# Sums over ordered rows by TensorE: two fp32r matmuls on a split operand in the place of one fp32 matmul

## The chip, the cores and the metric

The kernel runs on one core of a Trainium2 chip. The metric is the device time of one execution in microseconds (us). The time of the kernel before is the median of three runs, 2934.11 us. The engines are named as in the profile: PE is TensorE (matmuls and transposes), PEld its weight loads, DVE is VectorE, ACT is ScalarE, POOL is GpSimd, and SP issues most of the DMAs.

## The reference

Four graph-attention layers run over 32 independent graphs ("batches") of 512 nodes with 256 features, all in fp32. Each is `x = x + gat(relu(layernorm(x)))`. The last has two attentions inside, and the first of these has no mask. Cut to what matters here:

```python
def _gat(inp, adj_mask, W, a):
    h = jnp.matmul(inp, W)                       # (B, 512, 512) for this one
    f1 = jnp.matmul(h, a[:F_, 0])
    f2 = jnp.matmul(h, a[F_:, 0])
    e = jax.nn.leaky_relu(f1[:, :, None] + f2[:, None, :], ALPHA)
    if adj_mask is not None:
        e = jnp.where(adj_mask[None, :, :] > 0, e, NEG_INF)
    att = jax.nn.softmax(e, axis=2)
    return jax.nn.elu(jnp.einsum('bij,bjf->bif', att, h))
```

Without a mask, the weight of row j for node i depends only on whether `f1[i] + f2[j]` is positive: on one side it is one product of a factor of i and a factor of j, on the other side another. So if the rows of h are put in the order of f2, the whole attention of a node is one sum over the rows before a place in the order and one over the rows after it. The kernel uses this.

## The kernel before, in words

The 32 batches go through the layers in four streams (`NS = 4`), batch b in stream b mod 4. Each batch is a Python generator that hands over control at `yield`, and gives with it the time at which it wants to go on. `after_us` works this time out from a planner's count: `spent`, which `matmul` and `transpose` raise for every call, and a number of us written out by hand. A loop at the end always advances the stream whose time comes first. This fixes the order in which the program is written down. From there a scheduler sets the order of each engine's queue: instructions that were written earlier come first where their inputs are due by then, and others may be moved up in the meantime. A few DVE instructions are kept in the order written (`tc.keep_in_program_order`).

SBUF tiles come from pools by tag. Tiles of one tag share a fixed number of buffers, and a new one has to wait until the oldest is free. The tag `q` has three buffers of 2 x 256 fp32 values a partition. The ELUs of all streams use it: ACT writes an exponential into `q`, and DVE reads it. The tag `w` has four buffers. PSUM's eight banks are divided so that each active stream has two (`bank()`).

Batches 0 to 30 take the unmasked attention as `sort_attend`; batch 31 takes it as `attend`, with matmuls over the full weights. `sort_attend` does the following:

1. `project_half` makes the rows of h in two halves of 256 columns. Two more columns are put to each half, so that it has C = 258.
2. DVE and ACT count each row's place in the order. POOL scatters the rows to DRAM at those places (L607), and SP reads them back in order: partition p gets rows 4p to 4p+3 (`sums`, L614 and L615).
3. For each half, DVE adds up the four rows of a partition from the front (L627, L628) up to the total `tot` (L629). It then sums them from the back with factors (L630, L632) to `u`. PE carries these sums across partitions: `pv` is the sum of `tot` over all partitions before, by a triangle of 0 and 1 called `before` as the stationary operand. `pu` is the same with `u[:, 0, :]` over all partitions after, by `after`. ACT copies `pv` out (L640), DVE adds `pv` and `pu` to the rows (L641, L644, L646), and SP writes the result to a table in DRAM (L647, L648).
4. POOL gathers from the table the row that belongs to each node (L655), and DVE and ACT finish the attention (L670 to L675).

So the triangles are used twice for each half, four times a batch, and 31 batches make 62 matmuls with each. They are made once, in `setup`, which runs between the first steps of the streams. All matmuls in the profile appear on line 66, in the helper `matmul`, so they are told apart by their operands. The same holds for transposes (L70).

Of the other streams' work, what stands near the sums in the queues is the end of layer 2 (L405, L406), the normalization (L269 to L280), layer 1's factors and values (`both` L324, `v` L322 and L325), the attention weights `w` (L353), the first matmuls of layer 3 (`hT,WM`) and the weighted sums (`v,w`).

Of the kernel before, what the change touches and what calls it, by code (L numbers as in the profile page):

```python
# [18 lines left out]

FP = mybir.dt.float32  # L20
BF = mybir.dt.bfloat16
I32 = mybir.dt.int32
U32 = mybir.dt.uint32
AF = mybir.ActivationFunctionType
OP = mybir.AluOpType
# [3 lines left out]
P = 128  # L29
# [6 lines left out]
def fast(ctx, tc, flag, x, adj, w0, a0, w1, a1, w2, a2, mlp1_w, mlp1_b, mlp2_w, mlp2_b,  # L36
         w_fc, a_fc, w_hand, a_hand, out):
    nc = tc.nc
# [12 lines left out]
    const = ctx.enter_context(tc.tile_pool(name="const", bufs=1))  # L51
    work = ctx.enter_context(tc.tile_pool(name="work", bufs=2))
# [11 lines left out]
    def matmul(p, w, x, **flags):  # L64
        spent[0] += 4 * max(x.shape[-1], P)
        nc.tensor.matmul(p, w, x, **flags)  # L66

    def transpose(p, x, i, tied=False):
        spent[0] += 2 * P
        instruction = nc.tensor.transpose(p, x, i)  # L70
        if tied:
            tc.keep_in_program_order(instruction)
# [4 lines left out]
    def bank():  # L77

        own = [turn[0], *(i for i in range(NS) if i not in active and i != turn[0])]
        banks[0] += 1  # L80
        return psum.tile([P, N], FP, tag=f"b{own[banks[0] % len(own)]}", name="b", bufs=8 // NS)
# [46 lines left out]
    def fetch_w(w, a, name):  # L128

        kt, cols = w.shape[0] // P, w.shape[1]  # L130
        t = const.tile([P, kt, cols + 3], FP, name=name)
        wr = w.rearrange("(k p) f -> p k f", p=P)
        for c in range(0, cols, F):
            nc.sync.dma_start(t[:, :, c + (3 if c else 0):c + (3 if c else 0) + F], wr[:, :, c:c + F])
        return t, fetch_a(a, name + "a") if len(a.shape) == 2 else a

    def finish_w(fetched, alpha):
        t, a_cols = fetched

        def block(k, f):  # L140
            c = f * P + (3 if f * P >= F else 0)
            return t[:, k, c:c + P]

        scale_a(a_cols, alpha)
        for k in range(t.shape[1]):
            project(t[:, k, F:F + 3], block, k, a_cols)
            yield
# [4 lines left out]
    W0, _ = fetched0 = fetch_w(w0, a0_sb, "W0")  # L152
    adj_sb = work.tile([P, NT, N], I32, tag="w", name="adj", bufs=4)
    nc.sync.dma_start(adj_sb, adj.rearrange("(t p) j -> p t j", p=P))
# [24 lines left out]
    b2 = const.tile([P, KF], FP, name="bias2")  # L179
    diag = const.tile([P, NT], I32, name="diag")  # L180
    with nc.allow_non_contiguous_dma(reason="vectors onto partitions"):
# [4 lines left out]
    C = F + 2  # L186
# [8 lines left out]


    maskT = const.tile([P, NT, N], BF, name="maskT")
    before = const.tile([P, P], FP, name="before")
    after = const.tile([P, P], FP, name="after")
    band = const.tile([P, 2 * N - P], BF, name="band")  # L200
    differ = const.tile([P, 2], FP, name="differ")

# [4 lines left out]
    def setup():  # L207

        own = work.tile([P, NT, N], FP, tag="w", name="own", bufs=4)
        nc.vector.tensor_scalar(own, adj_sb, 0.0, None, op0=OP.is_gt)  # L210
        nc.gpsimd.affine_select(
            out=own, in_=own, pattern=[[P, NT], [-1, N]], base=0, channel_multiplier=1,
            compare_op=OP.not_equal, fill=1.0,
        )
        tc.keep_in_program_order(nc.vector.tensor_reduce(differ[:, 0:1], adj_sb, AX.XY, OP.min))
        nc.vector.tensor_scalar(differ[:, 0:1], differ[:, 0:1], 0.0, None, op0=OP.is_lt)
        for j in range(NT):
            turn[0] = NS - 1 - j % (NS - 1)
            p = bank()
            for t in range(NT):  # L220
                transpose(p[:, t * P:(t + 1) * P], own[:, t, j * P:(j + 1) * P], ident, j + t == 0)
            nc.scalar.copy(maskT[:, j, :], p)
        turn[0] = NS - 1
        yield
        yield from finish_w(fetched1, 0.01)


        least = small([1], "rden")
        nc.vector.tensor_reduce(least, diag, AX.X, OP.min)
        nc.vector.tensor_scalar(differ[:, 1:2], least, 0.0, None, op0=OP.is_le)  # L230
        nc.vector.tensor_copy(W2[:, :, :, :D], raw2.rearrange("p k (h d) -> p k h d", d=D))
        nc.vector.tensor_scalar_mul(A2v[:, :, 1:2], A2v[:, :, 0:1], -0.8)
        nc.vector.tensor_scalar_mul(A2v[:, :, 2:3], A2v[:, :, 2:3], 0.8)
        for k in range(KF):
            project(W2[:, k, :, D:], lambda k, f: raw2[:, k, f * P:(f + 1) * P], k, A2)
            yield
        yield from finish_w(fetched3, 0.2)

        for tri, sign in ((before, 1), (after, -1)):
            nc.vector.memset(tri, 1.0)  # L240
            nc.gpsimd.affine_select(
                out=tri, in_=tri, pattern=[[sign, P]], base=0, channel_multiplier=-sign,
                compare_op=OP.is_gt, fill=0.0,
            )
        ties = work.tile([P, 2 * N - P], FP, tag="w", name="ties", bufs=4)
        nc.vector.memset(ties, TINY)
        nc.gpsimd.affine_select(
            out=ties, in_=ties, pattern=[[-1, 2 * N - P]], base=N - P, channel_multiplier=1,
            compare_op=OP.is_gt, fill=0.0,
        )  # L250
        nc.vector.tensor_copy(band, ties)
        yield
        yield from finish_w(fetched4, 0.2)
# [277 lines left out]
    def attend(oT, b):  # L531
# [28 lines left out]
        mlp_in(oT, ys[-1], NT - 1)  # L560
        yield after_us(1)

    def sort_attend(oT, b):

        halves, ends = fc_values()
# [12 lines left out]
        p = bank()  # L578
# [5 lines left out]
        for t in range(NT):  # L584
            junk = work.tile([P, N], BF, tag="junk", name="junk", bufs=1)
            nc.vector.scalar_tensor_tensor(
# [10 lines left out]
        for t in range(NT):  # L597
            junk = work.tile([P, N], BF, tag="junk2", name="junk2", bufs=1)
            nc.scalar.activation(
# [4 lines left out]
        for c in range(2):  # L604
# [7 lines left out]
            u = flat[c].rearrange("p (t k) n -> p t k n", k=2)[:, :, 1, :]  # L612
# [6 lines left out]
        for c in range(2):  # L619
            yield sort  # L620
            sums = flat[c].rearrange("p (t k) n -> p t k n", k=2)
            u = sums[:, :, 1, :]

            T = small([NT], "T")
            tc.keep_in_program_order(nc.vector.tensor_copy(T, u[:, :, F + 1]))
            tot = work.tile([P, C], FP, tag="tot", name="tot", bufs=1)
            nc.vector.tensor_tensor(sums[:, 2, 0, :], u[:, 0, :], u[:, 1, :], op=OP.add)  # L627
            nc.vector.tensor_tensor(sums[:, 3, 0, :], sums[:, 2, 0, :], u[:, 2, :], op=OP.add)  # L628
            nc.vector.tensor_tensor(tot, sums[:, 3, 0, :], u[:, 3, :], op=OP.add)  # L629
            nc.vector.tensor_scalar_mul(u[:, 3, :], u[:, 3, :], T[:, 3:4])  # L630
            for t in (2, 1, 0):
                nc.vector.scalar_tensor_tensor(  # L632
                    u[:, t, :], u[:, t, :], T[:, t:t + 1], u[:, t + 1, :], op0=OP.mult, op1=OP.add
                )
            yield after_us(3)

            pv, pu = bank(), bank()
            matmul(pv[:, :C], before, tot, start=True, stop=True)
            matmul(pu[:, :C], after, u[:, 0, :], start=True, stop=True)
            nc.scalar.copy(sums[:, 0, 0, :], pv[:, :C])  # L640
            nc.vector.tensor_tensor(  # L641
                sums[:, 1:, 0, :], sums[:, 1:, 0, :], pv[:, None, :C].to_broadcast([P, NT - 1, C]), op=OP.add
            )
            nc.vector.tensor_tensor(u, u, pu[:, None, :C].to_broadcast([P, NT, C]), op=OP.add)  # L644
            q = 3 * P // 4
            nc.vector.tensor_tensor(tot[q:, :], tot[q:, :], pv[q:, :C], op=OP.add)  # L646
            nc.sync.dma_start(places[:, :, c, :], flat[c])  # L647
            nc.sync.dma_start(table[N:, c * C:(c + 1) * C], tot[P - 1:, :])  # L648
            sort = after_us(1)
# [14 lines left out]
        for t in range(NT):  # L664
            yield landed
            y, q = pair(), pair("q")
# [128 lines left out]
    p = bank()  # L795
# [7 lines left out]
def general(  # L803
# [52 lines left out]

    adj_sb = work.tile([P, NT, N], I32, tag="u", name="adj", bufs=4)
    nc.sync.dma_start(adj_sb, adj.rearrange("(t p) j -> p t j", p=P))
    m_pos = const.tile([P, NT, N], BF, name="m_pos")
    nc.vector.tensor_scalar(m_pos, adj_sb, 0.0, NEG, op0=OP.is_le, op1=OP.mult)  # L860
    m_nz = const.tile([P, NT, N], BF, name="m_nz")
    nc.vector.tensor_scalar(m_nz, adj_sb, 0.0, NEG, op0=OP.is_equal, op1=OP.mult)
# [335 lines left out]
def kernel(ctx: ExitStack, tc: tile.TileContext, *args):  # L1198
    nc = tc.nc
    keep = ctx.enter_context(tc.tile_pool(name="keep", bufs=1))  # L1200
    flag = keep.tile([1, 1], I32, name="flag")
    fast(tc, flag, *args)
# [30 lines left out]
```

## Time and profile before

| What | Value |
|---|---|
| Time, median of 3 runs | 2934.11 us (2930.95 to 2935.68) |
| Span of the profiled execution | 2929.6 us, 43083 instructions |
| The profiled execution's own time | not listed apart; the three runs' times are 1.4 to 6.1 us above the span |
| Granted TensorE clock over the span | 0.996 |
| POOL busy | 502.3 us, 515 instructions |
| Matmul records `b<-tot,before` and `b<-sums,after` | 124 each |
| Subtraction-like row: `tot` (L629), DVE, 128x258 fp32 | x62, median 421 ns |
| Copy of `pv` (L640), ACT, 128x258 fp32 from PSUM | x62, median 374 ns |
| Table writes (L647) | x62, 516 KB each |

The span goes from the first to the last instruction on the core. A row of the profile names the line, the engine, the operation, the tile written and the tiles read, the shapes and the count. After the bar come the busy time in us and the mean time of one in ns, and after a second bar the engine's idle time just before these instructions. PE's records overlap, since a matmul starts before the one ahead of it has ended; the time that PE gives to a matmul is read from the distance between starts. In a timeline the columns are start, duration, engine, line and operation, and in brackets the idle time before and what ended it. In the chain of waits the columns are start, length and the instruction.

### The profile page before, as it was taken

What the parts mean: (1) busy time and instruction counts of PE and PEld (TensorE: products, weight loads), DVE (VectorE), ACT (ScalarE), POOL (GpSimd) and SP (SyncE); (2) the same over time, 40 slices, a digit from 0 to 9 for tenths busy, and PEclk for the clock granted to TensorE, in tenths of its full rate; (3) what the DMA queues carried; (4) which work ended last, traced back from release to release, by engine and by line L of the source; (5) the groups of instructions that cost most, each with busy time, mean ns of one, the idle gap of its engine ahead of it and who ended that gap; (6) DMA issues with size and microseconds to landing.
All of it is one profiled execution on the core that took longest, in us unless ns stands there. A gap on an engine that the chain in (4) does not pass through costs nothing.

```text
span 2929.6 us, 43083 instructions
## 1 busy us (share of the span) xinstructions
PE 2858.9 (98%) x15177; PEld 2329.5 (80%) x15177; DVE 2219.9 (76%) x5676; ACT 1536.8 (52%) x3922; POOL 502.3 (17%) x515
## 2 busy tenths in 40 slices
PE   8999999999999999999999999999999999999998
PEld 6777887877888877888877888788887788877876
DVE  4677877778778778778778777787787787777764
ACT  4444455555555555555554556545555555555444
POOL 0011112112122111122021121111221111211220
PEclk9999999999999999999999999999999999999999
DMA  3033223233223333233332233222332322323230
GB/s 94 19 102 102 80 88 116 91 98 95 88 94 106 93 100 98 84 102 96 100 102 80 89 115 93 91 97 91 94 116 80 102 93 88 104 93 96 90 107 30
DMA packets 193182, 270.89 MB, mean 92 GB/s; under 512 B 17024, under 2 KB 156094, under 8 KB 192960
## 3 DMA queue, kind: packets, MB, share of 16 engines
q1 hardware_dynamic: 163200, 169.76, 18.5%
q0 software_dynamic: 29760, 98.30, 10.4%
q8 instruction: 123, 2.02, 0.3%
q14 instruction: 99, 0.81, 0.1%
HBM read 152.62 MB, written 115.39 MB: 91 GB/s over the span
## 4 chain that ended last, share of the span: by engine, by line
PE 82%; DVE 10%; ACT 4%; DMA 3%; issue 1%; SPq 0%; POOL 0%; DVEq 0%; POOLq 0%; ACTq 0%
PE b L66 75%; PE b L70 7%; DVE st L269 2%; DMA g<-table,at 2%; DVE sums L641 1%; DVE xn L280 1%; DVE x L406 1%; DVE y L405 1%; ACT v L325 1%; DVE sums L632 1%; ACT y L505 1%; ACT q L504 1%; DVE w L353 1%; ACT hT L290 1%; DVE tot L646 0%
## 5 line engine op out<-in xcount | busy, mean ns | idle before, releaser
L66 PE MATMUL b<-v,w 128*128 128x65 f32 (+1 forms) x7232 | 1218.0, 321 | 10.6 <-DVE w L353 10.5
L66 PEld LDWEIGHTS b<-v,w 128*128 128x128 f32 x7232 | 1050.0, 191 | 168.7 <-issue 56.1
L66 PE MATMUL b<-WFC,oT 128*128 128x256 f32 (+1 forms) x2048 | 495.2, 380 | 0.0
L66 PEld LDWEIGHTS b<-WFC,oT 128*128 128x128 f32 x2048 | 374.5, 189 | 49.3
L66 PE MATMUL b<-W,hT 128*128 128x259 f32 (+1 forms) x1536 | 388.8, 391 | 22.8 <-DVE v L463 14.1
L353 DVE SCALAR_TENSOR_TENSOR w<-b,v,maskT 128x512 f32<-128x512 f32 x512 | 369.4, 744 | 5.1 <-PE b L70 4.1
L607 POOL DMA_INDIRECT order<-v,at x248 | 277.0, 1117 | 490.7 <-DVE oT L730 152.3
L66 PEld LDWEIGHTS b<-W,hT 128*128 128x128 f32 x1536 | 285.3, 192 | 75.3 <-DVE v L463 17.1
L715 POOL TENSOR_TENSOR x<-x,y 128x512 f32<-128x512 f32 x62 | 87.8, 1416 | 1063.7 <-ACT y L713 950.0
L353 DVE SCALAR_TENSOR_TENSOR w<-spread,v,maskT 128x512 f32<-128x512 f32 x384 | 269.5, 742 | 0.0
L66 PE MATMUL b<-hT,WM 128*128 128x512 f32 x512 | 250.0, 599 | 0.7 <-ACT hT L290 0.7
L66 PE MATMUL b<-oT,WM 128*128 128x512 f32 x512 | 231.2, 594 | 0.0
L655 POOL DMA_INDIRECT g<-table,at x124 | 120.9, 975 | 642.8 <-ACT y L675 292.0
L387 DVE RECIPROCAL rden<-b 128x1 f32<-128x1 f32 (+1 forms) x516 | 77.3, 162 | 184.8 <-PE b L66 183.0
L529 ACT ACTIVATE v<-b,ends 128x256 f32<-128x256 f32 x256 | 118.8, 467 | 177.2 <-PE b L66 172.9
L269 DVE BATCH_NORM_STATS2 st<-x 128x6 f32<-128x256 f32 x512 | 193.3, 409 | 6.4 <-DMA x<-in_x_dram 4.1
L412 DVE TENSOR_TENSOR y<-q,y 128x512 f32<-128x512 f32 (+1 forms) x194 | 132.9, 685 | 82.9 <-ACT q L411 45.0
L339 ACT ACTIVATE oT<-b,bias 128x512 f32<-128x512 f32 x128 | 87.7, 686 | 182.7 <-PE b L66 182.0
L290 ACT ACTIVATE hT<-b 128x512 f32<-128x512 f32 x256 | 146.5, 592 | 70.3 <-PE b L70 70.2
L66 PEld LDWEIGHTS b<-oT,WM 128*128 128x128 f32 x512 | 97.5, 191 | 95.7 <-issue 92.4
L70 PE MATMUL b<-ident,xn 128*128 128x128 f32 x1024 | 147.4, 275 | 6.7 <-DVE xn L280 4.0
L70 PEld LDWEIGHTS b<-ident,xn 128*128 128x128 f32 x1024 | 123.7, 143 | 31.9 <-DVE xn L280 5.2
(143 smaller groups left out, 3748.1 us busy)
## 6 DMA issues: line engine op xcount, KB each, us to landing
table<-sums SPq DMA_DIRECT2D x62, 1032.0 KB
sums<-order SPq DMA_DIRECT2D x62, 516.0 KB
spread<-row SPq DMA_DIRECT2D x96, 256.0 KB
x<-in_x_dram SPq DMA_DIRECT2D x32, 512.0 KB
out_dram<-x SPq DMA_DIRECT2D x62, 256.0 KB
sums<-order SPq DMA_DIRECT2D x62, 129.0 KB
order<-v,at POOLq DMA_INDIRECT x248
g<-table,at POOLq DMA_INDIRECT x124
```

Of the source, the lines that this page charges most:

```text
L66: nc.tensor.matmul(p, w, x, **flags)
L70: instruction = nc.tensor.transpose(p, x, i)
L269: nc.vector.bn_stats(st[:, i, :], xt[:, t0 + i, :])
L290: nc.scalar.activation(hT[:, :, t0 * P:(t0 + 2) * P], p.rearrange("p (k n) -> p k n", k=KF), AF.Relu)
L339: nc.scalar.activation(o[:, f, :], p, AF.Relu, bias=bias[:, f:f + 1])
L353: w = nc.vector.scalar_tensor_tensor(wt[:, j, :], r, t_col(j), maskT[:, j, :], op0=OP.max, op1=OP.mult)
L387: nc.vector.reciprocal(r, den)
L412: nc.vector.tensor_tensor(r, q, r, op=OP.add)
L529: nc.scalar.activation(halves[c][:, t, :F], ps[:, :F], AF.Copy, scale=ends[:, t, 0:1])
L607: nc.gpsimd.indirect_dma_start(out=orders[c], out_offset=bass.IndirectOffsetOnAxis(ap=at[:, 0, t:t + 1], axis=0), in_=halves[c][:, t, :], ...
L655: nc.gpsimd.indirect_dma_start(out=g, out_offset=None, in_=table, in_offset=bass.IndirectOffsetOnAxis(ap=at[:, 1, t:t + 1], axis=0),)
L715: (nc.gpsimd if n == 2 else nc.vector).tensor_tensor(xr, xr, y, op=OP.add)
```

## The change

The triangles become tiles of the type fp32r. Each is made in fp32 in a buffer of the tag `q` first and then copied by DVE[...]. At each of the two places in the sums where a triangle is used, a new helper `add_up` takes the moving operand apart: ACT writes it as fp32r (`high`), DVE subtracts that from the original and writes the rest as fp32r (`low`), and two fp32r matmuls by the triangle are added up in the same PSUM bank. The two parts lie in one tile of the tag `q`. The planner's count in `matmul` stays as it was, so it counts the two matmuls as twice one.

```diff
+FR = mybir.dt.float32r
...
-    before = const.tile([P, P], FP, name="before")
-    after = const.tile([P, P], FP, name="after")
+    before = const.tile([P, P], FR, name="before")
+    after = const.tile([P, P], FR, name="after")
...
-        for tri, sign in ((before, 1), (after, -1)):
+        for where, sign in ((before, 1), (after, -1)):
+            tri = work.tile([P, P], FP, tag="q", name="tri", bufs=3)
             nc.vector.memset(tri, 1.0)
             nc.gpsimd.affine_select(
                 out=tri, in_=tri, pattern=[[sign, P]], base=0, channel_multiplier=-sign,
                 compare_op=OP.is_gt, fill=0.0,
             )
+            nc.vector.tensor_copy(where, tri)
...
+    def add_up(p, ones, x):
+        parts = work.tile([P, 2, C], FR, tag="q", name="parts", bufs=3)
+        high, low = parts[:, 0, :], parts[:, 1, :]
+        nc.scalar.copy(high, x)
+        nc.vector.tensor_tensor(low, x, high, op=OP.subtract)
+        matmul(p, ones, high, start=True, stop=False)
+        matmul(p, ones, low, start=False, stop=True)
...
             pv, pu = bank(), bank()
-            matmul(pv[:, :C], before, tot, start=True, stop=True)
-            matmul(pu[:, :C], after, u[:, 0, :], start=True, stop=True)
+            add_up(pv[:, :C], before, tot)
+            add_up(pu[:, :C], after, u[:, 0, :])
             nc.scalar.copy(sums[:, 0, 0, :], pv[:, :C])
```

## The prediction

> **What bounds the kernel now.** First the page's busy table and the shares of the chain that ended last:
>
> ```profile
> PE 2858.9 (98%) x15177; PEld 2329.5 (80%) x15177; DVE 2219.9 (76%) x5676; ACT 1536.8 (52%) x3922; POOL 502.3 (17%) x515
> PE 82%; DVE 10%; ACT 4%; DMA 3%; issue 1%; SPq 0%; POOL 0%; DVEq 0%; POOLq 0%; ACTq 0%
> ```
>
> TensorE (PE) is busy 98% of the span and is 82% of the chain. A busy PE need not be a full one, so next the groups by shape and the timeline, for the pitch at which matmuls follow each other:
>
> ```profile
> L66 PE MATMUL b<-tot,before 128*128 128x258 f32 x124 | 37.9, 387 | 0.0
> L66 PE MATMUL b<-sums,after 128*128 128x258 f32 x124 | 37.8, 386 | 0.1
> ```
> ```profile
> 1062.59 0.60 PE L66 MATMUL b<-tot,before 128*128 128x258 f32 x2
> 1063.02 3.20 PE L66 MATMUL b<-v,w 128*128 128x257 f32 x14
> 163.91 3.01 PE L66 MATMUL b<-v,w 128*128 128x65 f32 x26
> ```
>
> 31 batches sort, each has two halves, and each half one matmul by `before` and one by `after`: 62 of each, but 124 records. So one fp32 matmul is two records, and the pair holds PE from 1062.59 to 1063.02, 0.43 us. The busy column (37.9 + 37.8 = 75.7 us) counts overlapping records; by the pitch these sums cost 124 x 0.43 = 53.3 us, 1.8% of the span. The last row gives another pitch: 26 narrow records in 3.01 us, (3.01 - 0.27) / 25 = 0.110 us each.
>
> Third, what lies around these matmuls: the busy time by windows, and the chain in order of time.
>
> ```profile
> 1050.00:1055.00 5.00, 5.00 (x25) 4.13 (x24) 4.86 (x20) 4.39 (x18) 0.00 (x0) 1.00 0.02 3
> 1055.00:1060.00 5.00, 4.09 (x25) 3.28 (x24) 4.77 (x9) 1.97 (x5) 0.00 (x0) 1.00 0.00 0
> 1060.00:1065.00 5.00, 5.00 (x21) 3.59 (x19) 5.00 (x12) 1.43 (x3) 0.00 (x0) 1.00 0.62 211
> 1065.00:1070.00 5.00, 5.00 (x21) 3.61 (x20) 4.35 (x10) 2.00 (x5) 0.00 (x0) 1.00 0.00 0
> ```
> ```profile
> 1054.95 0.96 DVE sums L641
> 1055.91 0.40 DVE sums L632
> 1056.34 0.44 DVE tot L646
> 1056.80 0.49 DVE sums L632
> 1057.29 0.08 DVE both L324
> 1057.40 0.48 ACT v L325
> 1057.92 0.65 PE b L70 x4
> ```
>
> The columns after the window are PE, weight load, VectorE (DVE), ScalarE (ACT) and POOL. In the 20 us of the sums DVE is busy 18.98 us, and PE loses 0.91 us there. The chain says why: another batch's layer 1 needs `both` (L324), which stands on DVE behind this batch's sums. So the whole is bound by PE, but the place that is changed is the one where DVE is full.
>
> Last, PE's waits by place. The pattern repeats every four batches, 355.5 us apart (waits on `w` at 969.51 and 1325.05). In one such turn PE idles near the sums 0.79, 0.90, 0.22 + 0.17 and 0.23 + 0.17 us, 2.48 in all, 0.62 us a batch; elsewhere there is one wait of 1.1 to 2.9 us on `v` (L463).
>
> [...]
>
> **The change, part by part.**
>
> 1. *PE.* Each fp32 matmul goes (0.43 us), two fp32r ones come. The trace has no fp32r operation. Lower bound of the price: [...]no less than the load's 110 ns of the trace. Upper bound: fp32r runs like one of today's records, 215 ns, and two make 0.43 us: nothing is saved. [...] That is a choice, not a measurement. Gain: (0.43 - 2 x 0.11) = 0.21 us a site, by 124 sites = 26 us. Range: 26 down to 0.
>
> 2. *DVE.* One subtraction 128x258 a site. The row for `tot` (L629), the same operation and shape from SBUF, has a median of 421 ns[...]. 124 x 0.421 = 52.2 us, 1.68 us a batch, all in the window that is full.
>
> 3. *ACT.* One copy 128x258 from SBUF a site. Nearest row: L640, 374 ns out of PSUM[...]. ACT is 52% busy, 2 to 4.4 us of 5 in the windows: the time itself is hidden under PE.
>
> 4. *The new wait.* A site's PE instruction now comes after ACT and DVE. Per pass: about 0.38 + 0.42 us later than `tot` is there, and handing over twice. Behind the subtraction on DVE are L641, L632 and layer 1's `both`, for which ACT (L325) and then PE wait; behind the copy on ACT are L322 and L325. The order of each queue is made by the scheduler that places instructions when their inputs are due, so PE is given other streams' matmuls meanwhile (hT,WM and v,w at 1060 to 1067). Bounds: at best nothing; at worst all 1.68 us of DVE work a batch becomes PE idle. Of the two halves only the first stands ahead of a PE wait (1057.92; in the second, 1062 to 1067, PE has no idle although DVE is full). The first half's two subtractions are 0.84 us; I take half of that, since part of the stretch is filled from elsewhere: 0.42 us x 31 = 13 us. Range 0 to 52.
>
> 5. *Buffers and plan.* `parts` and the two triangles use the tag `q`, three buffers of 2064 instead of 2048 bytes. The `q` tiles' own life is a few us (ACT's exponential to the DVE sum, e.g. 1048.38 to 1050.4), some ten of them in 89 us, so four more of about 2 us seldom find all three taken. Price 0; if the cover is gone, ACT waits and with it 4. The planner counts 4 x 258 cycles for each matmul, twice as many now: 2 x 2064/2400 = 1.72 us later for what follows each step, 3.4 us a batch, in all streams alike. This shifts priorities, and nothing on the chip is longer for it; I put 0 with ±8 us, the size of a quarter microsecond a batch, for another interleaving. PSUM: `pv` and `pu` are held some 0.6 us longer in a stream that has no other work then: 0. DMAs, SP's and POOL's queues: none added, moved or passed; the table's two writes follow about 1 us later in a chain that has a planned wait of 9 us behind it. At the end the last batch doesn't sort; 0.
>
> 6. *Setup.* Two DVE copies 128x128, under 0.3 us each, in the first 60 us, where DVE is busy 26.4: 0.
>
> Sum: -26 + 13 = -13 us; the profiled execution's span goes from 2929.6 to 2917. Its own time isn't shown beside the span; the times of the runs, 2930.95 to 2935.68, are 1.4 to 6.1 above it, and the median 4.5. I take the sum over to the median: 2934.1 - 13 = 2921. No change is what stays within 0.2%, 5.9 us; a measurement of this kernel can tell about that much.
>
> **The rivals.**
>
> *All of it arrives.* The subtractions fit in DVE's later gaps (1.47 us busy of 5 at 1085). For it: PE idles only 0.62 us a batch here. Against: the chain through L641 and L632. 2934 - 26 = 2908. Chance 0.17.
>
> *A wash.* The extra idle eats the gain: 0.84 us a batch of wait against 4 x 0.21 = 0.84 of matmul. 2934. Chance 0.15.
>
> *DVE sets the pace of the sums.* Place: the first-in-first-out queue of DVE at L629 to L646, with a subtraction that also waits for ACT. Price: all 1.68 us a batch become PE idle, 52 - 26 = +26, 2960. It decides from 0.84 us of added idle a batch; between that and the full price lie 2940 to 2960. For it: 18.98 of 20 us. Against: PE kept running through 1060 to 1070 with DVE just as full. Chance 0.22.
>
> *fp32r isn't faster here.* [...]124 x (2 x 0.215) = 53.3 us, as before, the wait of 13 us remains: 2947. For it: no row excludes it. Chance 0.10.
>
> *The forecast,* most of it arrives, 2913 to 2928: 0.36.
>
> **How the numbers follow.** Faster: 0.36 + 0.17 = 0.53. Within 0.2%: 0.15. Slower: 0.22 + 0.10 = 0.32. The lower end 2902 is full arrival with 6 us of luck in the interleaving; the upper end 2954 takes in the wash, slow fp32r and most of the DVE case. The forecast's own range is 2908 to 2931.
>
> **What would show it.** Right: rows for fp32r of 128x258 x248 in all, at a pitch near 0.11 us; subtractions x124 near 421 ns[...]; PE's idle near the sums rising from 0.62 to about 1.0 us a batch; a four-batch turn of about 354 us. Wrong: a pitch of 0.2 or more; PE waits naming the subtraction, or L324, L325 and L353, of more than 1.5 us a batch; ACT waiting for a `q` buffer; new waits far from the sums, which would be the plan's doing.

## Result and the profile after

The changed kernel takes 3034.9 us (median of 4 runs, 3031.62 to 3039.72) against 2933.7 us before: ratio 1.0348, 95% interval 1.0333 to 1.0363. It is slower by 101 us, far outside the predicted range, on the side that was given 0.32. The profiled execution's span is 3030.5 us. Line numbers are those of each kernel: in the changed one most lines stand 1 to 3 further down, and those of the sums and the gathers 13.

The busy table and the shares of the chain after:

```profile
PE 2887.6 (95%) x15177; PEld 2336.0 (77%) x15177; DVE 2263.9 (75%) x5802; ACT 1581.9 (52%) x4046; POOL 507.5 (17%) x515
PE 70%; DVE 15%; ACT 7%; DMA 5%; issue 3%; POOL 0%; SPq 0%; DVEq 0%; POOLq 0%; ACTq 0%
```

PE's share of the chain falls from 82% to 70%. Span minus busy time was 70.7 us and is 142.9 us: PE has 72 us more idle. PE's busy time also rises by 29 us, although its matmuls were foreseen shorter.

First the matmuls themselves. The groups by shape, and the timeline at three starts:

```profile
L67 PE MATMUL b<-parts,after 128*128 128x258 f32 x124 | 55.0, 454 | 1.9 <-DVE parts L572 1.9
L67 PE MATMUL b<-parts,before 128*128 128x258 f32 x124 | 44.5, 408 | 0.0
```
```profile
1088.63 0.47 PE L67 MATMUL b<-parts,before 128*128 128x258 f32 x1
1088.94 0.28 PE L67 MATMUL b<-parts,after 128*128 128x258 f32 x1
1089.06 0.60 PE L67 MATMUL b<-v,w 128*128 128x257 f32 x2
```

An fp32r matmul is one record, and the next instruction starts 0.12 us after it (1088.94 to 1089.06; at full clock the median behind a second part is 0.122 us), close to the 0.11 us foreseen. The 0.31 us between the first two starts isn't the price of one: an fp32r matmul behind an fp32 one is recorded as starting some 0.03 us after it (the median), while two fp32 records in a row start 0.215 us apart; 0.215 - 0.03 + 0.12 is about the 0.31. The record itself lasts longer than one of fp32 (408 to 454 ns against 387), although its price is 0.12 us and not 0.215. The idle time ahead of them is 1.9 us in all: PE hardly waits for the parts.

Then PE's waits:

```profile
PE b L71 <- DVE y L415: 49.6, 18, 7.6
PE b L71 <- DVE xn L283: 23.7, 25, 1.8
```

They were 4.6 us (`y`) and 4.0 us (`xn`), so these two make 65 of the 72 us. The loss stands at two places where PE transposes something that DVE is late with. The first, in the timeline:

```profile
1145.58 0.43 DVE L640 TENSOR_TENSOR sums<-sums 128x258 f32<-128x258 f32 x1 [6.39 <-DMA sums<-order]
1145.92 0.42 DVE L500 TENSOR_TENSOR y<-b,rden 128x256 f32<-128x256 f32 x1
1146.26 0.42 DVE L641 TENSOR_TENSOR sums<-sums 128x258 f32<-128x258 f32 x1
1146.59 0.69 DVE L415 TENSOR_TENSOR y<-q,y 128x512 f32<-128x512 f32 x1
1147.33 1.11 PE L71 MATMUL b<-ident,y 128*128 128x128 f32 x4 [6.00 <-DVE y L415]
```

`y` of one batch needed only the exponential that ACT had ended at 1139.9. But on DVE it stands three rows behind another batch's first sums instruction (L640), which waits 6.39 us for its rows from DRAM. PE's next instruction transposes `y`, so PE stands still too. The DMA isn't later than before: from the last place found to L640 it is 1125.63 to 1145.58, 19.95 us, and in the kernel before 1021.31 to 1041.16, 19.85 us:

```profile
1041.16 0.43 DVE L627 TENSOR_TENSOR sums<-sums 128x258 f32<-128x258 f32 x1 [0.68 <-DMA sums<-order]
```

There DVE had other work until 0.68 us before the rows came, and no `y` that PE needed stood behind the sums.

The windows around it (PE, weight load, DVE, ACT, POOL, then the granted clock):

```profile
1140.00:1142.00 2.00, 1.33 (x7) 0.82 (x5) 0.00 (x0) 0.61 (x2) 1.05 (x2) 1.00 0.18 66
1142.00:1144.00 2.00, 0.00 (x0) 0.00 (x0) 0.00 (x0) 0.00 (x0) 0.07 (x1) 1.00 0.59 146
1144.00:1146.00 2.00, 0.00 (x0) 0.00 (x0) 0.42 (x2) 0.00 (x0) 0.00 (x0) 0.83 0.97 271
1146.00:1148.00 2.00, 0.67 (x3) 0.67 (x4) 2.00 (x7) 1.27 (x3) 0.00 (x0) 0.50 0.90 309
1148.00:1150.00 2.00, 2.00 (x8) 1.63 (x7) 2.00 (x5) 0.83 (x2) 0.00 (x0) 0.50 0.00 0
1150.00:1152.00 2.00, 2.00 (x7) 1.51 (x6) 2.00 (x8) 0.50 (x2) 0.00 (x0) 0.50 0.00 0
1152.00:1154.00 2.00, 2.00 (x17) 1.87 (x16) 2.00 (x5) 0.60 (x1) 0.00 (x0) 0.96 0.04 12
```

The clock falls to a half about 4 us into the idle time and comes back some 5 us after PE is at work again, so a wait is paid a second time as a slow, "busy" PE. Over the seven waits of this kind, 3.75 to 7.58 us long, it falls 3.4 to 4.8 us into the wait and comes back 2.9 to 5.7 us after it.

The second place is in the sums, 30 us later:

```profile
1175.79 1.23 DVE L657 TENSOR_TENSOR sums<-sums,b 128x1032 f32<-128x1032 f32 x1
1176.93 0.73 DVE L283 TENSOR_SCALAR xn<-x,mv,rs 128x256 f32<-128x256 f32 x2
1177.39 1.11 PE L71 MATMUL b<-ident,xn 128*128 128x128 f32 x4 [1.76 <-DVE xn L283]
```

The longest instruction of the sums stands ahead of another batch's `xn`, for which PE waits: ACT had the last input of `xn` ready at 1176.03, so 0.9 of the 1.76 us are the queue's. The clock is halved there once more (0.50 in 1178 to 1182), although PE has waited 1.05, 0.27 and 1.76 us only, with matmuls between. No wait there is as long as the 3.4 us after which it fell at `y`, so one long wait isn't all that halves it; what does was not taken apart. Both come once in every turn of four batches.

A table of turns puts the whole together. A turn is a seventh of the time from batch 0's first output write to batch 28's. Idle is the sum of PE's gaps in it; "lost clock" is the time outside these gaps, multiplied by the part of the clock that was not granted (in a gap it isn't counted); the rest is PE's own work, with whatever waits the records hide. All columns are us, from one profiled execution each, except the medians of the runs.

| Kernel | Median | Turn | Idle | Lost clock | Rest |
|---|---|---|---|---|---|
| before | 2933.7 | 355.9 | 4.5 | 0.2 | 351.1 |
| after | 3034.9 | 369.3 | 14.0 | 5.2 | 350.1 |
| e1_plan | 2991.2 | 364.1 | 9.7 | 2.2 | 352.2 |
| e2_noplan | 2929.7 | 355.8 | 6.3 | 0.5 | 349.0 |
| e4_work | 2936.9 | 356.4 | 5.1 | 0.4 | 350.9 |
| e5_high | 2907.8 | 353.4 | 5.7 | 0.9 | 346.8 |
| e6_gather_early | 2969.5 | 360.1 | 8.6 | 2.2 | 349.3 |
| e7_three_behind | 3109.9 | 377.9 | 16.2 | 10.8 | 351.0 |
| e8_half | 2978.2 | 361.8 | 8.9 | 0.9 | 352.0 |
| e9_twice | 3001.6 | 365.1 | 7.5 | 5.3 | 352.4 |
| e10_less | 2963.5 | 359.4 | 6.6 | 0.5 | 352.4 |
| e11_true | 2986.9 | 363.4 | 8.9 | 2.6 | 351.8 |
| e12_pool | 2946.4 | 357.8 | 6.9 | 0.7 | 350.3 |
| e13_split_early | 2922.1 | 353.5 | 4.8 | 0.2 | 348.4 |
| e14_plan_work | 3003.2 | 365.4 | 10.8 | 2.3 | 352.3 |
| e15_plan_high | 3012.8 | 366.8 | 15.1 | 4.5 | 347.2 |
| e16_split_first | 2918.5 | 353.7 | 5.0 | 0.2 | 348.5 |

From before to after a turn is 13.4 us longer: 9.5 of it idle, 4.9 lost clock, less 1.0 of work. The rest differs by up to 1.3 us between the kernels that issue the same instructions as the one before (e1_plan, e8_half, e9_twice and e10_less), so smaller differences in that column say little. The experiments ask what made the waits.

### The profile page after: what moved, and what is told of

Same layout as the page of the kernel before. It is cut to its first block, busy times and chain, and to the rows that moved or that the text cites. A ratio compares the mean times of both kernels' runs of the same rounds, so it can differ in the third digit from the quotient of the medians.

```text
span 3030.5 us, 43379 instructions
## 1 busy us (share of the span) xinstructions
PE 2887.6 (95%) x15177; PEld 2336.0 (77%) x15177; DVE 2263.9 (75%) x5802; ACT 1581.9 (52%) x4046; POOL 507.5 (17%) x515
## 4 chain that ended last, share of the span: by engine, by line
PE 70%; DVE 15%; ACT 7%; DMA 5%; issue 3%; POOL 0%; SPq 0%; DVEq 0%; POOLq 0%; ACTq 0%
PE b L67 64%; PE b L71 5%; DMA order<-v,at 2%; DVE w L356 2%; DMA g<-table,at 2%; DVE st L272 1%; DVE g L683 1%; DMA sums<-order 1%; DVE y L415 1%; DVE xn L283 1%; DVE junk L599 1%; DVE sums L654 1%; ACT q L414 1%; DVE v L466 1%; DVE y L408 1%
## 5 line engine op out<-in xcount | busy, mean ns | idle before, releaser
L67 PE MATMUL b<-v,w 128*128 128x65 f32 (+1 forms) x7232 | 1241.8, 323 | 15.9 <-DVE w L356 10.3
L67 PEld LDWEIGHTS b<-v,w 128*128 128x128 f32 x7232 | 1064.0, 193 | 191.8 <-issue 71.0
L67 PE MATMUL b<-W,hT 128*128 128x259 f32 (+1 forms) x1536 | 403.3, 401 | 24.3 <-DVE v L466 14.1
L356 DVE SCALAR_TENSOR_TENSOR w<-b,v,maskT 128x512 f32<-128x512 f32 x512 | 365.1, 744 | 11.6 <-PE b L71 9.8
L67 PEld LDWEIGHTS b<-W,hT 128*128 128x128 f32 x1536 | 292.0, 197 | 84.6 <-DVE v L466 20.7
L620 POOL DMA_INDIRECT order<-v,at x248 | 283.5, 1143 | 387.7 <-DVE w L356 99.8
L71 PE MATMUL b<-ident,xn 128*128 128x128 f32 x1024 | 156.4, 281 | 28.8 <-DVE xn L283 23.7
L687 ACT ACTIVATE q<-g,rden 128x512 f32<-128x512 f32 x124 | 89.3, 720 | 161.8 <-DVE rden L390 124.1
```

What stands on the lines that cost most here:

```text
L356: w = nc.vector.scalar_tensor_tensor(wt[:, j, :], r, t_col(j), maskT[:, j, :], op0=OP.max, op1=OP.mult)
L620: nc.gpsimd.indirect_dma_start(out=orders[c], out_offset=bass.IndirectOffsetOnAxis(ap=at[:, 0, t:t + 1], axis=0), in_=halves[c][:, t, :], ...
L687: nc.scalar.activation(q, z, AF.Exp, scale=rd)
```

## Experiments

Three theories at first. **PLAN**: the planner's count, doubled by `add_up`, puts the sorting batches later against the others. **WORK**: the copies and subtractions overload DVE and ACT. **ORDER**: whatever alters what the scheduler weighs gives another order, good or bad.

**e1_plan: the count alone**

```diff
             matmul(pu[:, :C], after, u[:, 0, :], start=True, stop=True)
+            spent[0] += 2 * 4 * C
```

> The kernel before with one line more: after the two fp32 matmuls of the sums the planner's count is raised by 2 x 4 x 258 cycles, as add_up's four matmuls raise it. No instruction differs. Theory PLAN (the planner's later due times, 1.72 us a step, make the bad interleaving): 3000 to 3060 us, with a DVE y (ELU sum of the unmasked attention) held 4 to 8 us behind a sums instruction that waits for its DMA, once in four batches. Theory WORK (the added copies and subtractions do it): 2934 within 6 us. Theory ORDER (any change of what the scheduler weighs gives another order, good or bad, and the loss isn't tied to one part): anything from 2920 to 3040, with waits at other places than in the changed kernel.

2991.2 us, ratio 1.0195 (1.0173 to 1.0217). The first row of PE's waits:

```profile
PE b L70 <- DVE y L412: 44.9, 17, 6.0
```

No instruction differs from the kernel before, and 58 of the 101 us are lost. In the order on DVE, `y` stands 3 rows behind the next batch's sums in every fourth batch, as in the changed kernel, and 14 or more ahead of them in the kernel before. PLAN is shown for more than half; it doesn't account for the rest (2991 against 3035).

**e2_noplan: the change without the doubled count**

```diff
         matmul(p, ones, high, start=True, stop=False)
-        matmul(p, ones, low, start=False, stop=True)
+        nc.tensor.matmul(p, ones, low, start=False, stop=True)
```

> The changed kernel, but the second matmul of add_up isn't counted by the planner, so that due times are those of the kernel before. PLAN: the loss goes and the matmuls' gain shows, 2905 to 2930 us. WORK: 3035 within 15 us. ORDER: another order again, 2920 to 3040, and the time goes with the waits of PE for y and xn and the half clock after them.

2929.7 us, ratio 0.9988 (0.9981 to 0.9996). One line that issues the same instruction takes 105 us off the changed kernel. The wait for `y` is gone, and at the top stands what the kernel before had there (`v`, 14.1 us):

```profile
PE b L67 <- DVE v L466: 18.2, 7, 3.3
```

**e4_work: the copies and subtractions alone**

The kernel before, with fp32 triangles, and with this `add_up` (shown against that of the changed kernel):

```diff
     def add_up(p, ones, x):
         parts = work.tile([P, 2, C], FR, tag="q", name="parts", bufs=3)
         high, low = parts[:, 0, :], parts[:, 1, :]
         nc.scalar.copy(high, x)
         nc.vector.tensor_tensor(low, x, high, op=OP.subtract)
+        matmul(p, ones, x, start=True, stop=True)
-        matmul(p, ones, high, start=True, stop=False)
-        matmul(p, ones, low, start=False, stop=True)
```

> The kernel before with the copies and subtractions of the change (124 of each, into tag q, never read by a matmul) and its fp32 matmuls on the whole operand. Planner's count as before. WORK: as the changed kernel without its gain, 3034 + 26 = 3060 us within 20. PLAN: near 2934, at most some 15 us above it. ORDER: 2930 to 3040, by how the waits fall.

2936.9 us, ratio 1.0012 (1.0002 to 1.0022). Some 100 us of added DVE and ACT work (by the changed kernel's 124 x 0.42 and 124 x 0.41 us) cost 3 us where the plan is that of before. WORK falls as the cause of the 101 us.

**e5_high: the high part alone, old count**

```diff
         nc.scalar.copy(high, x)
-        nc.vector.tensor_tensor(low, x, high, op=OP.subtract)
-        matmul(p, ones, high, start=True, stop=False)
-        matmul(p, ones, low, start=False, stop=True)
+        matmul(p, ones, high, start=True, stop=True)
```

> The changed kernel with the low part left out: one fp32r matmul a site[...], no subtraction (the sums are rounded: part of the computation is left out). Planner's count as before the change. PE gives up 124 x (0.43 - 0.11) = 40 us, DVE has nothing added. WORK: faster than before, 2895 to 2910 us. PLAN: 2895 to 2915. ORDER: 2895 to 3010, the gain of 40 us plus whatever waits the new order has.

2907.8 us, ratio 0.9907 (0.9884 to 0.9929). A gain on PE does arrive: 26 us of the 40 expected. By the table the rest of a turn falls by 4.3 us for 16 sites, 0.27 us a site in place of 0.32, and the idle time rises by 1.2.

Next, whether the mechanism at `y` is the whole of it. **QUEUE**: what stands behind the first sums on DVE sets the loss.

**e6_gather_early: one number of the plan, count still doubled**

```diff
-        yield after_us(9)
+        yield after_us(8)
         got, when, gs = [], [], []
```

> The changed kernel with one number of the plan changed: the wait written ahead of the gathers is 8 instead of 9 us (1.5 us earlier in due time). Every instruction is that of the changed kernel, and the count stays doubled. In the program's order on DVE, the last ELU sum y of the unmasked attention now stands 14 or more rows ahead of the next batch's first sums in all batches; in the changed kernel it stands 3 rows behind it in every fourth. Theory QUEUE (the loss is y held on DVE behind a sums instruction that waits for its DMA, with PE's transposes of y behind that, and the half clock that follows): 2920 to 2945 us, no wait for y above 2 us in the steady part. Theory WORK-IN-PLAN (a plan with the doubled count is slow because the stages drift apart, whatever stands behind what): stays within 20 us of 3034.

2969.5 us, ratio 1.0124 (1.0102 to 1.0146): between the two expectations. `y` is ahead of the sums and its wait is gone, and 65 us of the 101 with it. But PE's longest waits are now

```profile
PE b L67 <- DVE v L466: 39.5, 25, 4.0
```

layer 2's values, 39.5 us in 25 waits where e2_noplan has 18.2 in 7. QUEUE explains the wait for `y`, not the whole. In DVE's queue these waits are of the same kind, at another DMA:

```profile
1191.08 0.76 DVE L683 SCALAR_TENSOR_TENSOR g<-g,ends 128x516 f32<-128x516 f32 x1 [4.13 <-DMA g<-table,at]
1191.75 0.87 DVE L466 SCALAR_TENSOR_TENSOR v<-b,rs,v 128x256 f32<-128x256 f32 x2
```

The first instruction on a gathered row waits 4.13 us on DVE for its DMA, and `v`, for which PE waits 3.28 us, stands next behind it. The kernel before has this pair too, once a turn, for 2.0 of its 4.5 us of idle time; here it is 5.6 of 8.6 us, and so 3.6 of the 4.1 us that are added. This is read from the traces; no run took the place apart.

**e7_three_behind: `y` behind the sums in three of four batches**

```diff
-        sort = after_us(11)
+        sort = after_us(15)
         for c in range(2):
             yield sort
```

> The changed kernel with the plan's wait ahead of the sums raised from 11 to 15 us. In the order on DVE, y now stands 3 to 5 rows behind the next batch's first sums in three of four batches instead of one of four. QUEUE: three times the loss of the y waits; e1_plan's loss was 58 us for one in four, so 3100 to 3220 us, with PE waits for y of some 4 to 8 us three times a turn of four batches. WORK-IN-PLAN: within 30 us of 3034.

3109.9 us, ratio 1.06 (1.0578 to 1.0622), within QUEUE's range, but not for its reason:

```profile
PE b L67 <- DVE rden L390: 47.4, 15, 3.7
PE b L71 <- DVE y L415: 17.1, 6, 13.6
```

The long waits for `y` (13.6 and 1.9 us) come when the last batches end; in the turns there is none over 1 us. Mostly PE waits for a reciprocal (`rden`), and that stands ahead of the sums. One of the fifteen:

```profile
1084.75 0.75 DVE L683 SCALAR_TENSOR_TENSOR g<-g,ends 128x516 f32<-128x516 f32 x1
1086.53 0.16 DVE L390 RECIPROCAL rden<-b 128x1 f32<-128x1 f32 x1
1086.61 0.41 DVE L640 TENSOR_TENSOR sums<-sums 128x258 f32<-128x258 f32 x1
```

PE stands still from 1084.03 to 1086.76, and in this time DVE doesn't wait for a DMA: it works through other instructions that were ready. So it is in all fifteen. `y` stands behind the sums three times a turn, as planned, but DVE comes to the sums when their rows are there or nearly so (in the turns its longest wait for them is 1.7 us). That the time fell into QUEUE's range is luck. These waits have another cause: what DVE, at work, has in its queue ahead of what PE needs. The lost clock, 10.8 us a turn, is the largest of all runs.

**e8_half and e9_twice: smaller and larger errors of the count**

The line of e1_plan with 4 * C and with 4 * 4 * C.

> The kernel before with the planner's count raised by half as much as in e1_plan (4 x 258 cycles a step). y stands 14 or more rows ahead of the sums in all batches. QUEUE: 2925 to 2945 us. A loss that grows with the planner's error (theory DOSE): half of e1_plan's 58 us, 2963 within 10.

> The kernel before with the planner's count raised by twice as much as in e1_plan (16 x 258 cycles a step). y again stands 13 or more rows ahead of the sums in all batches. QUEUE: 2925 to 2950 us, although the planner is wronger than in e1_plan. DOSE: 2934 + 116 = 3050 us within 25.

2978.2 us (1.0154, 1.0131 to 1.0176) and 3001.6 us (1.0225, 1.0206 to 1.0245). Both theories miss. `y` is ahead of the sums in both, so QUEUE, as it was put, asked for some 2935. The loss rises with the count (0, 45, 58, 68 us for 0, 0.5, 1 and 2 times the error), but not in proportion, and by different waits. In e8_half it is layer 2's values in nearly every batch, once a turn before:

```profile
PE b L66 <- DVE v L463: 42.5, 28, 3.7
```

They stand behind the gathered row as in e6_gather_early, 6.1 of the 8.9 us of idle time a turn. In e9_twice it is `y` again, 20.6 us in 16 waits, with 5.3 us of lost clock a turn. Of the nine waits over 1 us, eight stand seven instructions behind a gathered row that DVE waited for, 1.8 to 3.1 us. So QUEUE named one DMA too few for these runs: the rows of the sums are one, the gathered rows another.

**e10_less and e11_true: the count too low, and the true count**

e10_less is the kernel before with `spent[0] -= 4 * C`; e11_true is the changed kernel with 2 * C for both matmuls of a site together, which is about what they take (0.215 us in the planner's count; two pitches are 0.24).

> The kernel before with the planner's count lowered by 4 x 258 cycles a step, the opposite of e8_half. Nothing else differs. ORDER: the time moves by more than 0.2% either way, with PE's waits at other places; no size can be named. DOSE in its wider form (the later the plan puts the sorting streams the worse, e8_half +45, e1_plan +58, e9_twice +68 us): at or below 2932, by up to 45 us. If the plan of the kernel before is a narrow best case, it is slower here too, 2940 to 2990.

> The changed kernel with the two fp32r matmuls counted as what they take by the profile's pitch, 2 x 258 cycles together: the due times of e10_less. If the due times set the time: e10_less minus what e2_noplan gained over the kernel before, 3 to 8 us. ORDER: within 15 us of e10_less.

2963.5 us (1.0114, 1.0088 to 1.014) and 2986.9 us (1.0194, 1.0167 to 1.0221). So the plan of before is the fastest of the five counts tried, and a count that is right about the chip makes it slower. The due times don't set the time alone, either: e11_true is 23 us above e10_less with the same ones, while e2_noplan was 4 us below the kernel before.

**e14_plan_work and e15_plan_high: the other 44 us**

e1_plan is 44 us faster than the changed kernel. e14_plan_work is e4_work, e15_plan_high is e5_high, each with the doubled count (`spent[0] += 2 * 4 * C`).

> e1_plan (fp32 matmuls, doubled count) with the change's copies and subtractions added, which no matmul reads. e1_plan was 2991 us and the changed kernel is 3035: 44 us more although its matmuls are shorter. If the added DVE and ACT work makes these 44 us under this plan: 3020 to 3065 us, with PE waiting for xn (L283 of the changed kernel) 1 to 2 us a piece in every fourth batch. If they come from PE's matmuls waiting for the parts: within 12 us of 2991.

> The changed kernel with the high part alone, one fp32r matmul a site and no subtraction ([...]part of the computation is left out), and with the count of the changed kernel (four matmuls a step). If the subtraction on DVE is what adds to e1_plan's loss: 2991 minus the 26 us that e5_high gained, 2955 to 2975. If the copies or the fp32r matmuls do: 3000 to 3040.

3003.2 us (1.0247, 1.0225 to 1.0269) and 3012.8 us (1.027, 1.0247 to 1.0294). The work adds 12 us to e1_plan (14 when each is taken against the kernel before of its own series), as much as was allowed for the other answer. e15_plan_high has no subtraction, and yet it is 22 us above e1_plan and has the largest idle time but one. Its second place is where the changed kernel's is, with a wait for `v` as the larger part (here too the long sums instruction stands ahead on DVE, from 1180.15 to 1181.36):

```profile
1179.57 0.33 PE L71 MATMUL b<-ident,xn 128*128 128x128 f32 x1 [1.10 <-DVE xn L283]
1182.67 2.02 PE L67 MATMUL b<-W,hT 128*128 128x259 f32 x8 [2.27 <-ACT v L328]
```

So the subtraction isn't what adds to the plan's loss. What e15_plan_high and the changed kernel have in common, and e14_plan_work lacks, are fp32r matmuls that come after ACT's copy, and with them another order at the sums; whether the type or the copy matters was not taken apart. Why the scheduler then puts the long sums instruction ahead of `xn` stays open.

**e12_pool, e13_split_early and e16_split_first: where the gain of 26 us went, with the old count**

e12_pool is e2_noplan with `nc.gpsimd.tensor_tensor` for the subtraction. The other two write the split ahead of the plan's wait:

```diff
             tot = work.tile([P, C], FP, tag="tot", name="tot", bufs=1)
...
+            halves_of = [split(tot), split(u[:, 0, :])]
             yield after_us(3)
             pv, pu = bank(), bank()
-            add_up(pv[:, :C], before, tot)
-            add_up(pu[:, :C], after, u[:, 0, :])
+            add_up(pv[:, :C], before, *halves_of[0])
+            add_up(pu[:, :C], after, *halves_of[1])
```

`split` holds the copy and the subtraction of `add_up`. In e16_split_first `split(tot)` stands straight after `tot` is made.

> e2_noplan with the subtraction on POOL in the place of DVE. Where did e2_noplan's 26 us go? If into DVE's full stretch: 52 us of DVE work are away and the time is 2905 to 2918. If into the wait for the parts or into fp32r matmuls that cost more than 0.11 us: 2925 to 2940; with POOL late behind its scatters, more.

> e2_noplan with the copies and subtractions written ahead of the plan's wait of 3 us, in the step that makes tot and u, so that the parts should be there when the matmuls' turn comes. If the wait for the parts took the gain: 2905 to 2920. If DVE's work or the price of fp32r did: 2925 to 2940.

> e13_split_early with the split of tot written still earlier, straight after tot is made and ahead of the factor sums of u. e13_split_early gained 10 us. If what is left of the 26 us stands in the wait for tot's parts: 2908 to 2918. If not: 2918 to 2926, or another order and worse.

e12_pool: 2946.4 us (1.0049, 1.0031 to 1.0067), slower: DVE has 52 us less to do (124 x 0.42) and nothing comes of it, and PE now waits for the parts:

```profile
PE b L574 <- POOL parts L572: 9.3, 31, 0.4
```

e13_split_early: 2922.1 us (0.9965, 0.9952 to 0.9979). e16_split_first: 2918.5 us (0.9951, 0.9935 to 0.9967). Both are faster than both kernels; the second gains 13 us, just above its expected 2908 to 2918. By the table the idle time comes down from 6.3 to 4.8 and 5.0 us a turn, close to the 4.5 of before, and the rest is 348.4 and 348.5. So the place of the split took about 1.4 us a turn of the gain, 11 us in 31 batches. What then remains is PE's own work, which falls by 2.7 us a turn and not by 3.4.

## Why the prediction was wrong

**The step that failed is 5**, the plan: "This shifts priorities, and nothing on the chip is longer for it; I put 0 with ±8 us". The 1.72 us a step was worked out rightly, and e1_plan shows that it costs 58 us by itself. The bound was a guess. In fact an order can put one batch's work behind another's DMA wait, for 6 us at a time (`y` behind L640), where ±8 us allowed 0.26 us a batch. Two things that the sum had no term for made it large: queues in which an unready instruction holds up a ready one (L640's 6.39 us ahead of `y`), seen in the prediction for DVE in the sums but not followed to other places, and the clock, which turned 9.5 us of added idle time a turn into 14.4 us.

**Step 1, right in kind, too large.** The pitch is 0.12 us. The author's estimate for it was 0.11, after the pitch of the narrow records before (0.110 us; their weight loads start 0.112 us apart); that trace has no fp32r matmul. What a site costs in place is the time from the start of the matmul ahead of it to the start of the one behind it, less the usual pitch of the first and PE's gaps (stretches at half clock left out): in the turns on average 0.46 us before (0.43 was taken), 0.29 in e2_noplan and 0.27 to 0.28 in e13_split_early and e16_split_first. So a site gains 0.17 to 0.19 us in place of 0.21, and 124 sites 21 to 23 us, not 26. Two pitches are 0.24 us; the other 0.03 to 0.05 us a site are most likely waits for the parts that the long records hide, which no run took apart. By the table, the gain is 0.13 (e2_noplan: 2.1 us a turn over 16 sites) to 0.17 us, which agrees within the scatter of its last column.

**Step 2, right:** subtractions x124 at 420 ns against 421. **Step 3, too low:** the copies take 406 and 408 ns against L640's 374; 124 of them are 50 us, where 374 ns would make 46. Both are hidden: e4_work, which carries them, is 3 us above the kernel before. **Step 6, right:** the two copies in `setup` take 227 and 210 ns.

**Step 4, right under the old plan:** idle time rises by 1.8 us a turn in e2_noplan, 0.45 us a batch, against 0.42. The cause given, the first half's subtractions on DVE, is not borne out: with them, but read by no matmul (e4_work), it rises by 0.6 us a turn, and without any (e5_high) by 1.2. (In e12_pool, where POOL does them, it is no smaller either, but there PE waits for POOL.)

**The step on buffers** (tag `q`): no wait for one was seen, though no run took it apart.

With the measured terms for the old plan the sum would have been -21 + 14 = -7, against e2_noplan's -4 us.

**The rival on the slower side** had the right place, a DVE queue at the sums, for one of the two stalls, but the wrong mechanism: not 1.68 us of subtractions a batch, since e4_work carries all of them for 3 us, but what stands behind what. Of the signs named for a wrong forecast one held: new waits far from the sums, "which would be the plan's doing". PE's idle time does rise by 2.4 us a batch, but its waits name `y` and `xn`, not the subtraction (1.9 us in the whole run) or the rows that were listed.

**What stays open:** why the plan of before leaves so few waits while its neighbours on both sides leave more, and the 44 us between e1_plan and the changed kernel, of which some 12 go with the added work and the others with the order at the sums. In e7_three_behind it stays open why DVE falls behind.

## What to carry to other kernels

Where a planner's count or a scheduler's weights set the order, look at what an edit does to the count before looking at the chip's work, and take the two apart: keep the due times when the instructions change (e2_noplan), and change the due times alone (e1_plan). In this kernel, with PE 98% busy, the edits that kept the due times moved the time by -26 to +12 us, and those that altered them cost 29 to 178 us. Look first at what stands in a queue behind an instruction that waits for a DMA, at every such DMA: here the sums' rows (6.0 us of idle time a turn in the changed kernel) and the gathered rows (2.0 us even before). It isn't all: in e7_three_behind the waits for `rden`, the longest in sum, have no DMA wait ahead of them. Operands that are made by other engines were here best made ahead of the wait that is there already (2918.5 us in e16_split_first against 2929.7 in e2_noplan).

## What the hardware showed that was not expected

A PE gap of 6.0 us cost about 2.4 us more by the halved clock (0.50 from some 4 us into the gap until 5 us after its end); over a turn of the changed kernel the lost clock is 5.2 us beside 14.0 us of idle time. Where gaps of 1.05, 0.27 and 1.76 us follow each other with little work between them, it was halved as well, once in each of the seven turns: in four within the last gap, in three 0.3 to 1.2 us after it. An fp32r matmul of 258 columns is recorded with 408 to 454 ns on average but gives way to the next after 0.12 us, so the busy column overstates it even more than for fp32 (386 to 387 ns, next after 0.215 us).
